# Two expert parts of 40 and 9 node tiles in place of 36, 12 and one tile computed densely

## The chip, the core and the metric

The kernel runs on one core of a Trainium2 chip. The metric is device time in microseconds (us), from launch to end, lower is better. The three timed runs shown took 4450.0 to 4450.73 us, their median is 4450.49 us.

## The reference

A stack of four layers works on 6250 nodes with 256 features and 106,250 edges, sorted by their target. Each layer reads a layer norm of `x` and adds its result to `x`: a graph convolution of the GIN kind, a slice attention, a GCN convolution, and a mixture of eight experts. The change touches the last one:

```
x_flat = x.reshape(-1, 256)
gate_logits = x_flat @ Wg + bg + bias                  # 6250 x 8
topk_vals, topk_idx = top_k(gate_logits, 2)
topk_w = softmax(topk_vals)
combine = (one_hot(topk_idx, 8) * topk_w[..., None]).sum(axis=1)
h = relu(einsum('td,edh->teh', x_flat, W1) + b1)       # W1: 8 x 256 x 512
y = einsum('teh,ehd->ted', h, W2) + b2                 # W2: 8 x 512 x 256
out = einsum('ted,te->td', y, combine)                 # two of eight experts count for each row
```

So for each row only two experts have a weight other than zero, and the kernel computes those two alone, except where the text below says otherwise.

## The kernel before

**Tiles.** Rows are taken in 49 tiles (NT) of 128 (P); the last one, tile 48, has 106 rows. An edge stage walks the tiles in order: GpSimd gathers 128 edge rows at a time (`msg`, L152; 831 gathers for each stage), VectorE builds 0/1 matrices (`hot`, L194), and TensorE sums the messages with three products each (`pa`, L173). The ring holds 10 gathered rows ahead. A tile's sum arrives in halves: each closes with row `s<-pa,ln` (L978) or L981.

**The third stage and its experts.** The GCN layer's sums and the experts share one loop (L1320 to L1342). While the sums of a tile run, seven slots (`between_products`, L1298) let other work in. A slot gives one step to the oldest *chain* (`choice`, L1004, one for two tiles) and half a block to the experts (`block_pieces`, L1280).

A chain makes the layer's output rows, normalizes them (`xn`), computes the gate logits (`pg`), picks two experts (L1042 to L1052), counts rows of each expert with two products (`pp`, L1075 and L1076), and so finds for every row two places in a table `XD` in DRAM (`place`). It takes seven steps. Then `send` (L1090) scatters the rows of `xn` to their places by indirect DMA from GpSimd, one for each tile and choice, and `advance` (L1118, some 28 small VectorE rows) works out which *blocks* of 128 rows of one expert are now full.

**Parts.** `XD` is divided into parts: part 0 has tiles 0 to 35, part 1 tiles 36 to 47. A part of T tiles has 2T + 7 blocks: 79 and 31. A block whose rows can't all be known before its part's last tile waits for it. So 18 blocks of each part become due only with its last `send`.

**A block.** `fetched` (L1170) loads on SP's queue the block's rows (`xd`) and its expert's weights (`weights_of`, L1159): W1 and W2 of 512 KB each, b1, and b2 as 128 KB. Up to four blocks are fetched ahead (AHEAD, L988), when a block ends or after a tile. `block_of` (L1206) transposes xd (`pt`, `xdT`), makes four column groups of the hidden layer (`ph`, L1195; `hT`, L1197) and the output (`py`, L1202; `yd`, L1203), and stores yd over the block's rows in `XD` (L1229).

**Combining.** Once all blocks of a part are stored, each of its tiles is combined: two indirect gathers (`g`, L1260) fetch its rows' two results, and two VectorE rows (L1265) add them to `xr` with their shares. The output store follows (`flush`, L1000). In the loop a tile is combined every eighth gather of msg (`beside`, L1270).

**The last tile.** Tile 48 belongs to no part. Its chain ends with its shares of all eight experts (`share`), and each expert is computed for the whole tile as one of eight *dense* blocks, without xd or a store; L1216 adds each to xr.

**The tail.** Behind the loop (L1343 on) what is left runs: the last `send`, the blocks still due, the dense blocks, with one step of the last chain and one tile's combining beside each half block; then what remains to be combined.

**Order.** SP, TensorE, ScalarE and VectorE run this stage in program order. GpSimd's indirect copies are kept in order by hand (`in_order`, L159). Thus a waiting instruction on SP holds back all loads and stores behind it, and one on GpSimd all gathers and scatters.

```
for upto, size in ((0.75, P), (1.0, P)):
    ts = [t for t in range(sum(map(len, parts)), NT - 1) if (t + 0.5) / (NT - 1) <= upto]
...
due.extend(fresh)
due.extend((None, e) for e in range(NE))
while due or ready or pending[0] is not None:
    next(last, None)
    next(block_pieces)
    if to_combine:
        combine(now[0] + 2)
    run_ends()
```

Of the kernel before, what the change touches and what calls it, by code (L numbers as in the profile page):

```python
# [9 lines left out]
F32 = mybir.dt.float32  # L10
# [3 lines left out]
OP = mybir.AluOpType  # L14
# [3 lines left out]
P = 128  # L18
# [3 lines left out]
def gin_transolver_gcn_moe(ctx: ExitStack, tc: tile.TileContext, a: dict, out: bass.AP):  # L22
# [13 lines left out]
    nc = tc.nc  # L36
    x, src, dst = a["x"], a["src"], a["dst"]
    N, D = x.shape
    E = src.shape[0]
    NT = -(-N // P)  # L40
# [17 lines left out]
    def rows_of(t):  # L58
        return min(P, N - t * P)
# [91 lines left out]
    def gather(msg, table, ix):  # L151
        return nc.gpsimd.indirect_dma_start(out=msg, out_offset=None, in_=table,  # L152
                                            in_offset=bass.IndirectOffsetOnAxis(ap=ix, axis=0))
# [217 lines left out]


    parts, Bs = [], []
    for upto, size in ((0.75, P), (1.0, P)):
        ts = [t for t in range(sum(map(len, parts)), NT - 1) if (t + 0.5) / (NT - 1) <= upto]
        if ts:
            parts.append(ts)
            Bs.append(size)
# [608 lines left out]

    TG, AHEAD = 2, 4  # L988
    outs = []
    share = keep.tile([P, NE], F32, name="share")  # L990
    s3s = {}

    def load_ahead(t):
# [10 lines left out]
    def choice(i, ts, sent_at):  # L1004
# [51 lines left out]
        def shares():  # L1056
            nc.scalar.activation(best[:, :J, 2], best[:, :J, 2], AF.Exp)
            nc.vector.tensor_scalar(best[:, :J, 3], best[:, :J, 2], 1.0, None, op0=OP.add)
            nc.vector.reciprocal(sh[:, :, 0], best[:, :J, 3])
            nc.vector.tensor_mul(sh[:, :, 1], best[:, :J, 2], sh[:, :, 0])  # L1060

        if i is None:
            shares()
            dense.append(xT)
            nc.vector.tensor_scalar(share, pick[0][:, 0, :], sh[:, 0, 0:1], None, op0=OP.mult)
            nc.vector.scalar_tensor_tensor(share, pick[1][:, 0, :], sh[:, 0, 1:2], share, op0=OP.mult, op1=OP.add)
            return


        both = w.tile([P, 4, NE], F32, name="both")  # L1070
        nc.vector.tensor_add(both[:, :J, :], pick[0][:, :J, :], pick[1][:, :J, :])
        yield
        yield
        pp = ps.tile([P, 2, 4, NE], F32, name="pp", tag="mm", bufs=3)
# [15 lines left out]
    def send(i, ts, xn):  # L1090

        for j, t in enumerate(ts):
            for c in range(2):
                ins = nc.gpsimd.indirect_dma_start(  # L1094
                    out=XD[i], out_offset=bass.IndirectOffsetOnAxis(ap=place[:, t, c:c + 1], axis=0),
                    in_=xn[:, j, :], in_offset=None)
                in_order(ins, False)
                for other in sent[i] + taken[i] + stored[i]:
                    tc.declare_no_dep(ins.ins, other, reason="no two rows go to one place")
                sent[i].append(ins.ins)  # L1100
        final = ts[-1] == parts[i][-1]
        which = advance(i, final)
        rows = 2 * P * (ts[-1] + 1 - parts[i][0])
        n = n_blocks[i] if final else max(0, -((NE * (Bs[i] - 1) - rows) // Bs[i]))
        fresh.extend((i, which, no, len(sent[i])) for no in range(n_due[i], n))
        n_due[i] = n
# [82 lines left out]
    def products(xdT, W1, W2, b1, b2):  # L1189

        hT = ew.tile([P, KH, P], F32, name="hT")
        for m in range(KH):
            p = ps.tile([P, 512], F32, name="ph", tag="mm", bufs=3)
            for k in range(KD):
                nc.tensor.matmul(p[:, :P], W1[:, k, m * P:(m + 1) * P], xdT[:, k, :P],  # L1195
                                 start=(k == 0), stop=(k == KD - 1))
            nc.scalar.activation(hT[:, m, :], p[:, :P], AF.Relu, bias=b1[:, m:m + 1])  # L1197
        yield
        yd = ew.tile([P, D], F32, name="yd")
        p = ps.tile([P, 512], F32, name="py", tag="mm", bufs=3)  # L1200
        for m in range(KH):
            nc.tensor.matmul(p[:, :D], hT[:, m, :], W2[:, m, :], start=(m == 0), stop=(m == KH - 1))  # L1202
        nc.vector.tensor_tensor(yd, p[:, :D], b2[:, 0, :], op=OP.add)  # L1203
        yield yd

    def block_of(i, got):  # L1206

        if i is None:
            e, got = got
            it = products(dense[0], *got)  # L1210
            next(it)
            yield
            yd = next(it)
            fetch_more()
            r, o = rows_of(NT - 1), xr[:, NT - 1, :]
            nc.vector.scalar_tensor_tensor(o[:r], yd[:r], share[:r, e:e + 1], o[:r], op0=OP.mult, op1=OP.add)  # L1216
            return
        fetch, r0, xd, *got = got
        pt = ps.tile([P, 512], F32, name="pt", tag="tr")
        for k in range(KD):  # L1220
            nc.tensor.transpose(pt[:, k * P:(k + 1) * P], xd[:, k * P:(k + 1) * P], ident)  # L1221
        xdT = ew.tile([P, KD, P], F32, name="xdT")
        nc.scalar.activation(xdT, pt[:, :D].rearrange("p (k n) -> p k n", k=KD), AF.Copy)
        yield
        it = products(xdT, *got)
        next(it)
        yield
        yd = next(it)
        ins = nc.sync.dma_start(XD[i][ds(r0, P), :], yd)  # L1229
        for other in taken[i]:  # L1230
            if other is not fetch:
                tc.declare_no_dep(ins.ins, other, reason="another block's rows")
        stored[i].append(ins.ins)
        fetch_more()
        left[i] -= 1
        if not left[i]:
            to_combine.extend((sums.n + CPT // 2, i, t) for t in parts[i])
# [2 lines left out]


    due, fresh, ready, left = [], [], [], {i: n for i, n in enumerate(n_blocks)}
    to_send, to_combine, dense, ends = [], [], [], []
    n_due = [0 for _ in parts]
    SLOTS = 7
    now = [0]
# [1 line left out]
    def fetch_more():  # L1248
        while len(ready) < AHEAD and due:
            b = due.pop(0)  # L1250
            ready.append((b[0], (b[1], weights_of(slice(b[1], b[1] + 1))) if b[0] is None else fetched(*b)))

    def combine(when):

        _, i, t = to_combine.pop(0)
        o = xr[:, t, :]
        gs = []
        for c in range(2):
            g = w.tile([P, D], F32, name="g", bufs=8)
            in_order(gather(g, XD[i], place[:, t, c:c + 1]))  # L1260
            gs.append(g)

        def end():
            for c in range(2):
                nc.vector.scalar_tensor_tensor(o, gs[c], share_of[:, t, c:c + 1], o, op0=OP.mult, op1=OP.add)  # L1265
            flush(4)
            outs.append((out[t * P:(t + 1) * P, :], o))
        ends.append((when, end))

    def beside(t):  # L1270
# [9 lines left out]
    def blocks():  # L1280

        while True:
            if pending[0] is not None:
                for _ in pending[0]:
                    pass
                pending[0] = None
            if ready:
                i, got = ready.pop(0)
                pending[0] = block_of(i, got)
                next(pending[0])  # L1290
                if i is not None:
                    yield
                    next(pending[0])
            yield

    block_pieces = blocks()
# [18 lines left out]
    def new_blocks():  # L1315
        due.extend(fresh)
        fresh.clear()
        fetch_more()

    sums.beside = beside  # L1320
    for i, ts_ in [*enumerate(parts), (None, [NT - 1])]:
        for q in range(0, len(ts_), TG):
            ts = ts_[q:q + TG]
            for t in ts:
                load_ahead(t)
                s = s3s[t]

                nc.vector.scalar_tensor_tensor(s, xr[:, t, :], ln3[:, 0, t:t + 1], s, op0=OP.mult, op1=OP.add)
                k = iter(range(SLOTS))

                def between():
                    n = next(k, None)
                    if n is not None:
                        between_products(t, n)

                now[0] = t * SLOTS
                sums(t, between, SLOTS)
                for n in k:
                    between_products(t, n)
                if t < NT - 1:  # L1340
                    new_blocks()
            chains.append(choice(i, ts, min(NCH, start(2 * ts[-1] + 2) + 3 * CPT // 2)))  # L1342
    last, = chains  # L1343
    for _, *rows in to_send:
        send(*rows)
    due.extend(fresh)
    due.extend((None, e) for e in range(NE))
    while due or ready or pending[0] is not None:
        next(last, None)
        next(block_pieces)  # L1350
        if to_combine:
            combine(now[0] + 2)
        run_ends()
    while to_combine or ends:
        if to_combine:
            combine(now[0] + 2)
        run_ends()
    outs.append((out[(NT - 1) * P:N, :], xr[:rows_of(NT - 1), NT - 1, :]))
    flush(0)
    late.close()  # L1360

# [22 lines left out]
```

## Time and profile before

| | us |
|---|---|
| median of the timed runs | 4450.49 |
| the profiled execution | 4515.05 |
| its span, first to last instruction | 4513.4 |
| GpSimd busy | 2578.6 (57%) |
| TensorE busy, matmul | 3133.2 (69%) |
| VectorE, ScalarE busy | 1532.2 (34%), 788.2 (17%) |
| msg gathers (L152), 2493 | 2359.7, 947 ns each |
| scatters XD<-xn (L1094), 96 | 94.7, 986 ns each |
| gathers g<-XD (L152), 96 | 93.8, 977 ns each |
| first row of stage 3's sums (L978) | 2800.6 |
| last msg gather starts | 4280.65 |

Times in the profile count from the first instruction. The profiled execution is longer than the timed runs, so shares and differences are read from it, not totals. Busy shares are means over stages with different limits; mean granted TensorE clock is 0.817 of full speed, mean DMA traffic 231 GB/s. A row is named by line, engine and operation, then output<-inputs by the program's names. In a bracket stands the idle time of the engine just before a row and what ended it.

### The profile page before, as it was taken

Reading aid. Unit: us, or ns where it says so; the run is one execution under the profiler, and the core shown is the slowest. Engines: PE = TensorE matmul, PEld = TensorE weight load, DVE = VectorE, ACT = ScalarE, POOL = GpSimd, SP = SyncE. Lnnn points to the kernel's source line nnn. Section 1 sums busy time; section 2 is a strip of 40 time slices with the busy share of each in tenths; the row PEclk is TensorE's granted clock in tenths of the full one; section 3 lists DMA queues with packets and bytes.
Section 4 is the critical chain, followed back from the end, with each engine's and each line's share of the span. In section 5 each row is a group of like instructions: output and inputs, shape, how many; then the busy total and the mean of one; then the engine's idle time right before and its main releaser. Section 6 shows DMA issues by size and latency. Waiting matters only on the chain. (4 is left out here: it accounts for less than half of the span.)

```text
span 4513.4 us, 45778 instructions
## 1 busy us (share of the span) xinstructions
PE 3133.2 (69%) x14516; PEld 2025.4 (45%) x14592; DVE 1532.2 (34%) x3891; ACT 788.2 (17%) x1496; POOL 2578.6 (57%) x2719
## 2 busy tenths in 40 slices
PE   2577777777874777878767876566666666677567
PEld 1233343433442444434434454345555555566456
DVE  6122222222231433433434454333333332333332
ACT  4011111111120111111111123011212221122122
POOL 3666666666646666666666502665665555555642
PEclk6688888888987898988989977677778777788779
DMA  6676666666668888888888755467766676687678
GB/s 210 190 227 215 215 197 206 210 214 208 195 210 289 296 295 301 304 293 289 297 289 292 248 165 178 136 189 220 225 206 207 216 222 215 215 263 219 194 239 257
DMA packets 497447, 1044.56 MB, mean 231 GB/s; under 512 B 79469, under 2 KB 294607, under 8 KB 497200
## 3 DMA queue, kind: packets, MB, share of 16 engines
q0 software_dynamic: 182064, 678.86, 47.8%
q1 hardware_dynamic: 308656, 353.08, 24.0%
q10 hardware_dynamic: 6480, 9.63, 0.6%
q8 instruction: 117, 1.92, 0.2%
q14 instruction: 130, 1.06, 0.1%
HBM read 878.42 MB, written 162.92 MB: 231 GB/s over the span
## 5 line engine op out<-in xcount | busy, mean ns | idle before, releaser
L152 POOL DMA_INDIRECT msg<-T,srcT x2493 | 2359.7, 947 | 1682.4 <-issue 763.0
L173 PE MATMUL pa<-msg,hot 128*128 128x256 bf16 (+2 forms) x7404 | 1492.0, 342 | 540.7 <-DMA msg<-T,srcT 395.1
L173 PEld LDWEIGHTS <-hot 128*128 128x128 bf16 x7479 | 804.8, 108 | 1142.0 <-issue 742.6
L1195 PE MATMUL ph<-xdT,W 128*128 128x128 f32 x1760 | 287.4, 315 | 197.6 <-ACT hT L1197 85.6
L194 DVE SCALAR_TENSOR_TENSOR hot<-dstT,node 128x1152 bf16<-128x1152 f32 (+2 forms) x297 | 373.1, 1258 | 23.8 <-PE pa L173 12.9
L1195 PEld LDWEIGHTS ph<-xdT,W 128*128 128x128 f32 x1760 | 252.8, 219 | 232.5 <-ACT hT L1197 97.5
L1202 PE MATMUL py<-W,hT 128*128 128x256 f32 x944 | 264.9, 425 | 25.4 <-issue 13.8
L622 DVE TENSOR_TENSOR dinv<-dinv,pa 128x1 f32<-128x1 f32 x145 | 22.3, 153 | 714.2 <-PE pa L173 460.8
L1197 ACT ACTIVATE hT<-ph,b1e 128x128 f32<-128x128 f32 x472 | 165.9, 367 | 449.7 <-remote 161.9
L835 PE MATMUL ptok<-xn,sw 128*128 128x257 f32 (+1 forms) x392 | 125.1, 458 | 157.1 <-DVE sw L827 63.7
L670 PE MATMUL p<-W2a,h2T 128*128 128x512 f32 x392 | 199.8, 651 | 33.9 <-issue 18.0
L1202 PEld LDWEIGHTS py<-W,hT 128*128 128x128 f32 x944 | 190.5, 215 | 64.8 <-issue 22.6
L663 PE MATMUL p<-h1T,W1b 128*128 128x512 f32 (+2 forms) x448 | 204.0, 599 | 19.5 <-ACT h1T L657 13.1
L835 PEld LDWEIGHTS ptok<-xn,sw 128*128 128x128 f32 (+1 forms) x392 | 84.8, 227 | 195.7 <-issue 74.7
L152 POOL DMA_INDIRECT g<-XD,place x96 | 93.8, 977 | 125.0 <-DMA XD<-yd 54.8
L1203 DVE TENSOR_TENSOR yd<-py,b2e 128x256 f32<-128x256 f32 x118 | 49.9, 423 | 306.6 <-PE py L1202 177.4
L1015 PE MATMUL pn<-Wg,sT 128*128 128x256 f32 x196 | 82.2, 592 | 83.6 <-issue 44.6
L655 PE MATMUL p<-h0T,W1a 128*128 128x512 f32 (+2 forms) x224 | 129.8, 711 | 7.3 <-issue 4.0
L663 PEld LDWEIGHTS p<-h1T,W1b 128*128 128x128 f32 x448 | 87.5, 212 | 103.8 <-issue 83.2
L670 PEld LDWEIGHTS p<-W2a,h2T 128*128 128x128 f32 x392 | 78.0, 211 | 121.6 <-issue 103.7
L1094 POOL DMA_INDIRECT XD<-xn,place x96 | 94.7, 986 | 62.5 <-issue 46.1
L235 DVE TENSOR_TENSOR s<-s,pa 128x512 f32<-128x512 f32 x49 | 33.6, 685 | 269.0 <-PE pa L173 146.7
(306 smaller groups left out, 3059.6 us busy)
## 6 DMA issues: line engine op xcount, KB each, us to landing
W<-in_L_ffn_W SPq DMA_DIRECT2D x236, 512.0 KB
XD<-zeros SPq DMA_DIRECT2D x100, 512.0 KB
msg<-T,srcT POOLq DMA_INDIRECT x2493
T<-tp SPq DMA_DIRECT2D x49, 384.0 KB
b2e<-in_L_ffn_b SPq DMA_DIRECT2D x118, 128.0 KB
xd<-XD SPq DMA_DIRECT2D x110, 128.0 KB
XD<-yd SPq DMA_DIRECT2D x110, 128.0 KB
S<-s SPq DMA_DIRECT2D x49, 256.0 KB
```

The source lines that it names most:

```text
L152: return nc.gpsimd.indirect_dma_start(out=msg, out_offset=None, in_=table, in_offset=bass.IndirectOffsetOnAxis(ap=ix, axis=0))
L173: nc.tensor.matmul(pa[:, :n], hot, msg[:, s * F:s * F + n], start=(start and s == 2), stop=(stop and s == 1))
L194: nc.vector.scalar_tensor_tensor(hot[:, :n, :], dstT[:, c0:c0 + n, None].to_broadcast([P, n, P]), float(k * HALF), node2[:, k % 2, None, : ...
L655: nc.tensor.matmul(p[:, :T], W1a[:, k, m * P:(m + 1) * P], h0T[:, k, :T], start=(k == 0), stop=(k == KD - 1))
L663: nc.tensor.matmul(p[:, :T], W1b[:, k, m * P:(m + 1) * P], h1T[:, k, :T], start=(k == 0), stop=(k == KH - 1))
L670: nc.tensor.matmul(p, h2T[:, k, j * P:(j + 1) * P], W2a[:, k, :], start=(k == 0), stop=(k == KH - 1))
L835: nc.tensor.matmul(p[:, :D + 1], sws[j][:r, m * P:(m + 1) * P], xn[:r, j, :], start=(j == 0), stop=(j == J - 1))
L1015: nc.tensor.matmul(p[:, :D], sT[:, k, j * P:(j + 1) * P], Wg3[:, k, :], start=(k == 0), stop=(k == KD - 1))
L1094: ins = nc.gpsimd.indirect_dma_start(out=XD[i], out_offset=bass.IndirectOffsetOnAxis(ap=place[:, t, c:c + 1], axis=0), in_=xn[:, j, :], in ...
L1195: nc.tensor.matmul(p[:, :P], W1[:, k, m * P:(m + 1) * P], xdT[:, k, :P], start=(k == 0), stop=(k == KD - 1))
L1197: nc.scalar.activation(hT[:, m, :], p[:, :P], AF.Relu, bias=b1[:, m:m + 1])
L1202: nc.tensor.matmul(p[:, :D], hT[:, m, :], W2[:, m, :], start=(m == 0), stop=(m == KH - 1))
```

## The change

Parts are formed over all 49 tiles, with a limit of 0.81: part 0 has tiles 0 to 39, part 1 tiles 40 to 48. The numbers of blocks become 87 and 25, the dense blocks are gone. The last tile's chain is a chain like all others; rows past the 106 count as zero in `both`, and its scatters, gathers, sums and output store have 106 rows. In the tail, all chains that are left take one step in each round, and one waiting `send` is made in a round, after which its blocks are fetched at once.

```diff
-    for upto, size in ((0.75, P), (1.0, P)):
-        ts = [t for t in range(sum(map(len, parts)), NT - 1) if (t + 0.5) / (NT - 1) <= upto]
+    for upto, size in ((0.81, P), (1.0, P)):
+        ts = [t for t in range(sum(map(len, parts)), NT) if (t + 0.5) / NT <= upto]
...
-        if i is None:
-            shares()
-            dense.append(xT)
-            nc.vector.tensor_scalar(share, pick[0][:, 0, :], sh[:, 0, 0:1], None, op0=OP.mult)
-            nc.vector.scalar_tensor_tensor(share, pick[1][:, 0, :], sh[:, 0, 1:2], share, op0=OP.mult, op1=OP.add)
-            return
...
-        nc.vector.tensor_add(both[:, :J, :], pick[0][:, :J, :], pick[1][:, :J, :])
+        r = rows_of(ts[-1])
+        if r < P:
+            nc.vector.memset(both[:, :J, :], 0.0)
+            if J > 1:
+                nc.vector.tensor_add(both[:, :J - 1, :], pick[0][:, :J - 1, :], pick[1][:, :J - 1, :])
+            nc.vector.tensor_add(both[:r, J - 1, :], pick[0][:r, J - 1, :], pick[1][:r, J - 1, :])
+        else:
+            nc.vector.tensor_add(both[:, :J, :], pick[0][:, :J, :], pick[1][:, :J, :])
...
+            r = rows_of(t)
             for c in range(2):
                 ins = nc.gpsimd.indirect_dma_start(
-                    out=XD[i], out_offset=bass.IndirectOffsetOnAxis(ap=place[:, t, c:c + 1], axis=0),
-                    in_=xn[:, j, :], in_offset=None)
+                    out=XD[i], out_offset=bass.IndirectOffsetOnAxis(ap=place[:r, t, c:c + 1], axis=0),
+                    in_=xn[:r, j, :], in_offset=None)
...
-        if i is None:
-            e, got = got
-            it = products(dense[0], *got)
...
-            nc.vector.scalar_tensor_tensor(o[:r], yd[:r], share[:r, e:e + 1], o[:r], op0=OP.mult, op1=OP.add)
-            return
...
-            in_order(gather(g, XD[i], place[:, t, c:c + 1]))
-            gs.append(g)
+            in_order(gather(g[:r], XD[i], place[:r, t, c:c + 1]))
+            gs.append(g[:r])
...
-    for i, ts_ in [*enumerate(parts), (None, [NT - 1])]:
+    for i, ts_ in enumerate(parts):
...
-                if t < NT - 1:
-                    new_blocks()
+                new_blocks()
...
-    last, = chains
-    for _, *rows in to_send:
-        send(*rows)
-    due.extend(fresh)
-    due.extend((None, e) for e in range(NE))
-    while due or ready or pending[0] is not None:
-        next(last, None)
+    while chains or to_send or due or ready or pending[0] is not None:
+        for it in list(chains):
+            if next(it, chains) is chains:
+                chains.remove(it)
+        if to_send:
+            send(*to_send.pop(0)[1:])
+            new_blocks()
         next(block_pieces)
         if to_combine:
             combine(now[0] + 2)
...
-    outs.append((out[(NT - 1) * P:N, :], xr[:rows_of(NT - 1), NT - 1, :]))
```

More of the change, by code (lines that the diff above doesn't have):

```diff
@@ L989, in gin_transolver_gcn_moe @@
     outs = []
-    share = keep.tile([P, NE], F32, name="share")
     s3s = {}
@@ L1206, in block_of @@
     def block_of(i, got):
-        if i is None:
-            e, got = got
-            it = products(dense[0], *got)
[L1211 to L1215, printed above, removed]
-            nc.vector.scalar_tensor_tensor(o[:r], yd[:r], share[:r, e:e + 1], o[:r], op0=OP.mult, op1=OP.add)
-            return
         fetch, r0, xd, *got = got
@@ L1242, in gin_transolver_gcn_moe @@
     due, fresh, ready, left = [], [], [], {i: n for i, n in enumerate(n_blocks)}
-    to_send, to_combine, dense, ends = [], [], [], []
+    to_send, to_combine, ends = [], [], []
     n_due = [0 for _ in parts]
@@ L1250, in fetch_more @@
             b = due.pop(0)
-            ready.append((b[0], (b[1], weights_of(slice(b[1], b[1] + 1))) if b[0] is None else fetched(*b)))
+            ready.append((b[0], fetched(*b)))
     def combine(when):
         _, i, t = to_combine.pop(0)
-        o = xr[:, t, :]
+        r = rows_of(t)
+        o = xr[:r, t, :]
         gs = []
@@ L1259, in combine @@
             g = w.tile([P, D], F32, name="g", bufs=8)
-            in_order(gather(g, XD[i], place[:, t, c:c + 1]))
-            gs.append(g)
+            in_order(gather(g[:r], XD[i], place[:r, t, c:c + 1]))
+            gs.append(g[:r])
         def end():
             for c in range(2):
-                nc.vector.scalar_tensor_tensor(o, gs[c], share_of[:, t, c:c + 1], o, op0=OP.mult, op1=OP.add)
+                nc.vector.scalar_tensor_tensor(o, gs[c], share_of[:r, t, c:c + 1], o, op0=OP.mult, op1=OP.add)
             flush(4)
-            outs.append((out[t * P:(t + 1) * P, :], o))
+            outs.append((out[t * P:t * P + r, :], o))
         ends.append((when, end))
@@ L1290, in blocks @@
                 next(pending[0])
-                if i is not None:
-                    yield
-                    next(pending[0])
+                yield
+                next(pending[0])
             yield
```

## The prediction

> **What bounds the kernel now.** I read three views of the last sixth of the run: the start of row s<-pa,ln (L978, one per node tile), stage windows, and the timelines of SP and POOL. From tile 8 on, the third aggregation runs with three expert blocks beside one tile and one beside the next; from 3019.5 to 3951.8 us thirty such tiles take 932.3 us, 31.08 each. The program order of TensorE and the starts of yd<-py (L1203) give the blocks between them: 89 before the last product of row pa at 4300 us, 29 behind it.
>
> ```profile
> 4117.14 0.48 DVE L978 SCALAR_TENSOR_TENSOR s<-pa,ln,s 128x256 f32<-128x256 f32 x1 [1.71 <-PE pa L173]
> 4263.13 0.47 DVE L978 SCALAR_TENSOR_TENSOR s<-pa,ln,s 128x256 f32<-128x256 f32 x1
> 4303.07 0.48 DVE L978 SCALAR_TENSOR_TENSOR s<-pa,ln,s 128x256 f32<-128x256 f32 x1
> ```
>
> These are tiles 43, 47 and 48 (columns: start, length). Tiles 43 to 46 take 146.0 us, 36.5 each, with nine blocks only; tiles 38 to 42, with seventeen, took 165.3, 33.1 each. The four are those beside which the g gathers of part 0 run (nine tiles' pairs up to tile 47).
>
> The stage windows of the last 561.6 us (columns: stretch, length, busy us of PE, PEld, DVE, ACT and POOL, then granted clock, DMA share and GB/s):
>
> ```profile
> 3951.80:4117.10 165.30, 127.65 (x782) 108.64 (x780) 58.22 (x222) 43.04 (x105) 90.59 (x96) 0.87 0.81 252
> 4117.10:4263.10 146.00, 91.16 (x520) 74.16 (x520) 48.72 (x169) 25.95 (x60) 86.85 (x93) 0.76 0.64 195
> 4263.10:4303.10 40.00, 22.45 (x102) 17.30 (x99) 13.16 (x52) 7.47 (x14) 14.22 (x15) 0.63 0.71 219
> 4303.10:4345.30 42.20, 26.10 (x118) 22.32 (x118) 15.83 (x66) 10.79 (x26) 23.29 (x24) 0.70 0.62 193
> 4345.30:4406.10 60.80, 43.46 (x208) 35.53 (x208) 17.46 (x41) 14.59 (x40) 29.77 (x31) 0.80 0.89 276
> 4406.10:4460.60 54.50, 47.50 (x270) 38.92 (x269) 8.63 (x20) 18.71 (x51) 3.40 (x4) 0.97 0.92 281
> 4460.60:4513.40 52.80, 28.34 (x159) 24.96 (x157) 17.84 (x40) 9.36 (x26) 24.27 (x24) 0.83 0.74 235
> ```
>
> See that the tail from 4303.1 us has no gathers of msg, yet takes 210.3 us: it is the blocks that were left. Once it runs (rows five and six) DMA is 0.89 to 0.92 busy, so transfers set its pace. SP and POOL show its two edges:
>
> ```profile
> 4295.78 0.51 SPq L1002 DMA_DIRECT2D out<-xr  x1
> 4311.35 0.34 SPq L1229 DMA_DIRECT2D XD<-yd  x1
> 4317.74 0.72 SPq L1177 DMA_DIRECT2D xd<-XD  x1
> 4322.01 0.69 SPq L1161 DMA_DIRECT2D W<-in_L_ffn_W  x1
> ```
> ```profile
> 4409.47 0.95 POOL L152 DMA_INDIRECT g<-XD,place  x1 [0.30 <-issue]
> 4465.18 0.94 POOL L152 DMA_INDIRECT g<-XD,place  x1 [54.76 <-DMA XD<-yd]
> ```
>
> Between 4294.8 and 4322.0 us no weight is asked for: SP first waits for a block's yd, then xd waits for the last scatters (POOL, the last of them at 4307.38). And part 1's combining starts at 4465.18 us, 4.6 us behind the last store of yd (4460.59); the eight dense blocks run beside its 24 gathers.
>
> **The change, part by part.** *In the loop.* Blocks before the last pa stay 89, but part 0 ends at tile 40, so its backlog (17 blocks in five tiles) moves from tiles 38 to 42 to tiles 42 to 46, its last blocks are done at the loop's end, and no g gather is left in the loop. Tiles 38 to 41: 4 x 31.08 = 124.3; tiles 42 to 46: 165.3 as measured for the same blocks; tile 47 kept at 40.0 (it has two blocks for one, but loses a combined tile). Sum for tiles 38 to 46: 289.6 against 311.3, **21.7 us less**. I take all the excess of tiles 43 to 46 as the combining's; what else it could be is the second rival. Bounds: 5 and 32 less (32 if tile 47 too falls to 33).
>
> *Tail, start.* Block 92 (the fourth of the tail) has its yd at 4345.32, 42.2 us in. The fetch of 92 now stands ahead of the store of 89 on SP, so it waits for the scatters alone: a gain of 0 to 8. But tile 48 is scattered too: the fetch of block 96 waits on SP for its two scatters, and behind it stand all later weights, stores and outputs, hence every later block. Its chain ended at 4335.6 us before; the prefix product, place and POOL's two scatters come one block later, some 4348, landed some 10 us on (4307.38 to 4317.74 at the first such wait). Four blocks are in hand, and 23.3 us pass from W's issue to yd (4322.01 to 4345.32): cost 0 to 8. The two are set against each other: 0.
>
> *Tail, middle.* All 40 tiles of part 0 are now combined here, one per half block, so 20 blocks have gathers beside them. Such a block took (4406.09 - 4345.32) / 8 = 7.6 us; one without (yd 4418.76 to 4445.49, five blocks) 5.3. Blocks 93 to 107: 15 x 7.6 = 114.0. The last four have no weights left to load: 4 x 5.3 = 21.2. The last yd is at 42.2 + 114.0 + 21.2 = 177.4, its store 0.4 later.
>
> *Tail, end.* Nothing runs beside part 1's combining: 4.6 for the store to land, 17 gathers at 1.25 (0.95 and 0.30 issue), and from the last gather's start to the end 9.7 as now (4503.66 to 4513.4): 35.6. A gather's buffer is awaited only eight on (bufs 8), 10 us, so the gathers don't wait for DVE.
>
> *106 rows.* The rule that speaks against the change: the Trainium skill, "DMA: Bandwidth & Descriptors", section "Why a DMA increments its semaphore by 16 and not by 1", lets a copy use the largest number of engines up to 16 that divides the rows; for 106 that is 2. The trace agrees for the store of the last tile's output:
>
> ```profile
> 4508.90:4511.70 2.80, 0.00 (x0) 0.00 (x0) 0.00 (x0) 0.00 (x0) 0.00 (x0) 0.50 0.13 37
> ```
>
> 0.13 of 16 engines at 37 GB/s, where 128-row rows had 276. That store is last in both kernels. But the scatters and gathers of tile 48 are new copies of 106 rows. By the g row of 128 they cost nothing extra; by the rule each last gather takes some 2.5 us longer (108.5 KB at 37 GB/s is 2.9). No 106-row indirect copy is in the trace (the page names an exception for some copies from POOL); by shape the store is nearest: **+2**, ends 0 and 5.
>
> So the tail is 177.8 + 35.6 + 2 = 215.4 against 210.3: **5.1 us more**. That six blocks fewer (118 to 112; each 1.18 MB of weights and b2e, 4.3 us at 276 GB/s) don't shorten it: 24 of the g gathers and outputs of loop tiles move in, the dense blocks' cheap pace (eight in 40 us) goes, and the end has no cover.
>
> *Costed at nothing:* one more advance on DVE (4303.47 to 4307.59, 4.1 us) and the memset and add into both, DVE being busy 29% in the tail; without that cover, 5. Removed: ten small DVE rows of the dense part, ACT's 24 hT rows, hidden as well. Fills of XD grow from 100 to 102, each 0.5 MB, in the first stage beside gathers: 0, at most 5 if its DMA (0.66 busy) were the limit.
>
> Sum: -21.7 + 5.1 = -16.6 on the profiled 4515.05 us (span 4513.4). The runs' median, 4450.49, is 1.4% shorter than the profiled execution; scaled, -16.4: **4434.1**.
>
> **Rivals.**
> - *More gain:* tile 47 falls to 33 (-7), and the tail's middle runs at 6.4 as blocks 92 to 96 (6.7) and 99 to 102 (5.9) did on average (15 x 1.2 = 18 less): 41 less, 4410. Against it: 276 GB/s in the middle window.
> - *No loop gain:* tiles 44, 46 and 47 are long for late weights (TensorE idled 12.9 us before ph in tile 44) and low clock (0.76, 0.63), not for combining. Then tiles 42 to 46 take 36.5 each, 182.5 + 124.3 = 306.8, 4.5 less; with the tail's +5.1: 4451, no change. For it: a g pair is 2.5 us of POOL, POOL was 0.59 busy there. Against: these are the only long tiles.
> - *Slower, the second gate:* SP's hold for tile 48's scatters isn't covered but repeats the first one in full, 27.2 us from weight to weight (4294.8 to 4322.0), in a tail that DMA paces. -16.6 + 27.2 = +10.6: 4461. It takes back all gain from 16.6, and decides for slower from 25.5. For it: yd's gap of 19.6 us at the first gate (blocks 89 to 90). Against: then 22 us passed with the fetch queue not filled, now four blocks are fetched first.
> - *Not what it says:* excluded; the two programs' order on TensorE shows 118 blocks to 112 and 29 to 23 behind the last pa.
>
> **Numbers.** 0.2% (8.9 us) is about what a measurement of this kernel can tell from no change. Forecast 0.58 (0.52 faster, 0.05 same, 0.01 slower); more gain 0.14, all faster; no loop gain 0.15 (0.10 same, 0.05 slower, if a gate comes on top); second gate 0.13 (0.03 same, 0.10 slower). So faster 0.66, same 0.18, slower 0.16. Forecast's own range 4420 to 4448; to hold the rivals but for their outer halves, 4412 to 4462.
>
> **What would show it.** Right: no g row before the last msg gather; tiles 38 to 41 at 31 and 42 to 46 at 33 us; last pa 20 us earlier; the last store of yd 178 us behind tile 48's L978; the end 36 us behind that store. Wrong: tiles 42 to 46 at 36 or more; a gap of weights on SP over 15 us a second time; gathers g waiting at the end; blocks beside combining at over 8 us.

## The result, and the profile after

The changed kernel takes 4438.17 us (median of 20 runs, 4412.16 to 4473.14) beside 4456.67 us for the kernel before (20 runs, 4444.54 to 4475.54). The medians differ by 18.5 us. The comparison's own ratio is 0.9956, 95% interval [0.9937, 0.9974]: 19.6 us less, between 11.6 and 28. The forecast was 16.4 us less.

The profiled execution of the changed kernel took 4425.39 us (span 4423.7, mean clock 0.831). It can't be set against the 4515.05 us of before as a whole: 32 of the 89.7 us between the two spans lie ahead of stage 3, where only two fills of `XD` were added (2800.6 us to its first sum before, 2768.6 now). Another 30 lie in tiles 8 to 37, whose work is the same (31.08 us a tile before, 30.07 now). So the stages are compared, and even they are read from an execution that ran 3% faster where nothing was changed.

Starts of L978 in the changed kernel, tiles 43, 47 and 48 (columns: start, length):

```profile
4052.11 0.48 DVE L978 SCALAR_TENSOR_TENSOR s<-pa,ln,s 128x256 f32<-128x256 f32 x1 [0.78 <-PE pa L173]
4177.72 0.48 DVE L978 SCALAR_TENSOR_TENSOR s<-pa,ln,s 128x256 f32<-128x256 f32 x1 [2.54 <-remote]
4214.24 0.48 DVE L978 SCALAR_TENSOR_TENSOR s<-pa,ln,s 128x256 f32<-128x256 f32 x1
```

Tiles 43 to 46 now take 125.6 us for 146.0, and tile 47 36.5 for 40.0. The stage windows of the changed kernel (stretch, length, busy us of PE, PEld, DVE, ACT and POOL, granted clock, DMA share, GB/s): tiles 38 to 41, tiles 42 to 46, tile 47, the tail to yd of block 92, to block 107, to the last store, the end, and the last output's transfer alone:

```profile
3899.10:4018.80 119.70, 79.71 (x476) 65.61 (x476) 43.09 (x157) 24.60 (x56) 72.63 (x76) 0.81 0.70 218
4018.80:4177.70 158.90, 122.33 (x776) 106.06 (x776) 58.65 (x222) 43.47 (x105) 89.69 (x94) 0.88 0.83 256
...
4177.70:4214.20 36.50, 25.48 (x141) 20.88 (x140) 10.82 (x45) 8.83 (x18) 12.28 (x13) 0.73 0.73 222
4214.20:4253.50 39.30, 26.38 (x133) 23.21 (x134) 19.60 (x98) 12.02 (x29) 18.90 (x19) 0.79 0.56 170
4253.50:4364.60 111.10, 76.64 (x397) 63.06 (x395) 32.73 (x77) 26.89 (x76) 65.66 (x68) 0.88 0.93 296
4364.60:4387.60 23.00, 16.81 (x86) 13.70 (x86) 5.62 (x13) 5.86 (x17) 0.00 (x0) 0.93 0.78 245
4387.60:4423.70 36.10, 0.00 (x0) 0.00 (x0) 8.72 (x18) 0.00 (x0) 18.26 (x18) 0.54 0.41 119
4418.20:4422.50 4.30, 0.00 (x0) 0.00 (x0) 0.45 (x1) 0.00 (x0) 0.00 (x0) 0.50 0.09 25
```

See that the backlog of part 0 (second row) runs at 31.8 us a tile with TensorE the busiest, that the tail's middle (fifth row) stands at 0.93 of DMA and 296 GB/s, and that of the compute engines only GpSimd and VectorE work in the last 36 us.

SP's queue at the two gates, the waits for scatters:

```profile
4204.77 0.38 SPq L1163 DMA_DIRECT2D W<-in_L_ffn_W  x1
...
4207.23 0.36 SPq L1219 DMA_DIRECT2D XD<-yd  x1
4222.38 0.71 SPq L1177 DMA_DIRECT2D xd<-XD  x1
4224.52 0.00 SPq L1161 DMA_DIRECT2D W<-in_L_ffn_W  x1
...
4252.85 0.34 SPq L1165 DMA_DIRECT2D b1e<-B  x1
4253.40 0.59 SPq L1167 DMA_DIRECT2D b2e<-in_L_ffn_b  x1
4260.82 0.70 SPq L1177 DMA_DIRECT2D xd<-XD  x1
4261.63 0.38 SPq L1161 DMA_DIRECT2D W<-in_L_ffn_W  x1
4263.68 0.71 SPq L1163 DMA_DIRECT2D W<-in_L_ffn_W  x1
4267.25 0.69 SPq L1165 DMA_DIRECT2D b1e<-B  x1
4271.44 0.00 SPq L1167 DMA_DIRECT2D b2e<-in_L_ffn_b  x1
4272.14 0.70 SPq L1001 DMA_DIRECT2D out<-xr  x1
4274.24 0.69 SPq L1219 DMA_DIRECT2D XD<-yd  x1
...
4278.77 0.00 SPq L1161 DMA_DIRECT2D W<-in_L_ffn_W  x1
```

The fetch of block 92 stands ahead of stores and leaves at 4222.38; no weights were asked for in 19.7 us (4204.77 to 4224.52). The second gate is there too: the fetch of block 96 leaves at 4260.82, and the store of block 92's yd, ready at 4253.9, leaves only at 4274.24. What that costs is seen at VectorE's row of block 94:

```profile
4275.69 0.42 DVE L1203 TENSOR_TENSOR yd<-py,b2e 128x256 f32<-128x256 f32 x1 [6.56 <-remote]
```

It waits for two things. The tile yd has two buffers, so block 94 needs the one that block 92's store reads. And TensorE's py of this block, which by the profile's model ends at 4268.55, updates its semaphore only at 4275.67. Both engines are slow in this stretch; the last section returns to it.

GpSimd's two scatters of tile 48, and its last gathers:

```profile
4249.32 1.57 POOL L1094 DMA_INDIRECT XD<-xn,place  x1 [14.76 <-ACT hT L1197]
4251.20 1.57 POOL L1094 DMA_INDIRECT XD<-xn,place  x1 [0.31 <-issue]
...
4390.31 0.95 POOL L152 DMA_INDIRECT g<-XD,place  x1 [26.73 <-DMA XD<-yd]
...
4410.31 1.57 POOL L152 DMA_INDIRECT g<-XD,place  x1 [0.30 <-issue]
4412.19 1.56 POOL L152 DMA_INDIRECT g<-XD,place  x1 [0.30 <-issue]
```

The second gate's rows were sent at 4251.20. Part 1's combining starts 2.7 us behind the last store (4387.6), and goes, with never more than the usual 0.30 us between gathers, to the two gathers of 106 rows, which keep GpSimd for 1.57 us each in place of 0.95.

### The profile page after: what moved, and what is told of

It reads as the page before. It is cut to its first block, busy times and chain, and to the rows that moved or that the text cites. A ratio compares the mean times of both kernels' runs of the same rounds, so it can differ in the third digit from the quotient of the medians.

```text
span 4423.7 us, 45587 instructions
## 1 busy us (share of the span) xinstructions
PE 3063.0 (69%) x14455; PEld 1970.8 (45%) x14456; DVE 1531.8 (35%) x3910; ACT 780.1 (18%) x1474; POOL 2587.1 (58%) x2723
## 5 line engine op out<-in xcount | busy, mean ns | idle before, releaser
L173 PE MATMUL pa<-msg,hot 128*128 128x257 bf16 (+2 forms) x7479 | 1494.5, 340 | 567.9 <-DMA msg<-T,srcT 473.0
L1202 PE MATMUL py<-W,hT 128*128 128x256 f32 x896 | 238.5, 411 | 14.4 <-ACT hT L1197 7.9
L1202 PEld LDWEIGHTS py<-W,hT 128*128 128x128 f32 x896 | 174.9, 207 | 44.5 <-ACT hT L1197 11.3
L815 PE MATMUL pl<-Weff,xnT 128*128 128x512 f32 x196 | 112.9, 664 | 24.8 <-issue 13.9
L236 DVE TENSOR_TENSOR s<-s,pa 64x512 f32<-64x512 f32 x48 | 33.2, 692 | 249.1 <-PE pa L173 114.2
```

The source lines that it names most:

```text
L173: nc.tensor.matmul(pa[:, :n], hot, msg[:, s * F:s * F + n], start=(start and s == 2), stop=(stop and s == 1))
L815: nc.tensor.matmul(p, xnT[:, k, j * P:(j + 1) * P], Weff[:, k, :], start=(k == 0), stop=(k == KD - 1))
```

## The experiments

Twelve experiments ran, in three groups, each timed beside the kernel before: its median is 4532.69 us (59 runs) in the first group, 3991.35 (43 runs) in the second, 4524.52 (52 runs) in the third. The record doesn't tell which chip a group ran on. Ratios are to before in the same group. The stages below come from one profile each; groups one and three are close in pace and stand together, with the two first profiles. "Sum" is from tile 38 to the end, and "end" from the last store of yd (with dense blocks, that end also holds them).

| kernel | tiles 38-46 | tile 47 | tail | of it end | sum |
|---|---|---|---|---|---|
| before (first profile) | 311.3 | 40.0 | 210.3 | 52.8 | 561.6 |
| b_copy (before) | 307.8 | 40.6 | 210.8 | 52.2 | 559.2 |
| after (first profile) | 278.6 | 36.5 | 209.5 | 36.1 | 524.6 |
| a_again (after) | 296.7 | 38.3 | 225.5 | 36.0 | 560.5 |
| a_third (after) | 291.4 | 39.7 | 217.8 | 36.2 | 548.9 |
| b_tail_combine | 290.3 | 38.7 | 222.3 | 56.2 | 551.3 |
| b_tail_combine_wf | 279.3 | 37.2 | 220.3 | 55.0 | 536.8 |
| b_40_8_dense | 288.9 | 41.2 | 218.9 | 49.7 | 549.0 |
| a_36_13 | 305.4 | 39.9 | 217.0 | 46.0 | 562.3 |
| a_wf_g128 | 293.7 | 38.2 | 222.9 | 32.4 | 554.8 |

Read the three rows of the changed kernel first: their sums differ by 36 us, more than the change brings. One profile shows where a stage's time goes, not whether the kernel is faster; for that the timed ratios stand. Means agree with them (before 560.4, after 544.7, 15.7 us less), but this is weak support: with such a spread the mean of three sums is known to some 10 us (an estimate from the three), so that the agreement is in part luck.

**a_again and a_third: the changed kernel once more.** No edit.

> The changed kernel once more, as a yardstick beside the next three. Theory (combining moved out of the loop): about 0.9956 of before; tiles 42 to 46 near 1.06 of the ordinary tiles, tail some 210 us, 36 us of it after the last store. Any rival expects the same total.

> The changed kernel unchanged, beside the three others on their chip, as their base. Expected from its two earlier comparisons (0.9956 and 0.9972): ratio to before 0.995 to 0.998. If what the change does depends on the chip, it falls outside.

Measured: 4521.75 us, ratio 0.9972 [0.9952, 0.9991], and 4509.27 us, 0.9966 [0.9948, 0.9983]. With 0.9956 that is three comparisons, each faster, by 12.7 to 19.6 us. Each is known to some 9 us either way, and so are the other ratios of groups one and three.

**b_tail_combine: the kernel before, but no tile is combined in the loop.**

```diff
-        if n % (CPT // 2) == 0 and to_combine and to_combine[0][0] <= n:
-            combine(t * SLOTS + (n - start(2 * t)) * SLOTS // CPT + 2)
```

> The kernel before, but no tile is combined in the loop: all 36 of part 0 wait for the tail, nothing else changes. Theory (combining beside the sums made tiles 43 to 46 long): these four fall from 36.5 to 31 or 32 us each, 20 us less; nine more tiles combined beside tail blocks cost 9 x 1.15 = 10 us; total 10 us less, 0.998 of before. Rival (late weights and a low clock made them long): they stay at 36, total 10 us more, 1.002. Rival (fewer blocks are the whole gain): no faster than before, 1.000 to 1.002.

Measured: 4523.66 us, ratio 0.9958 [0.9938, 0.9979] (the two plain medians give 0.9980, which lies outside the comparison's interval; for the changed kernel beside it they give 0.9976, and the comparison 0.9972). The size is thus uncertain between 9 and 19 us. By either reading two lines taken away, with the old parts and the dense last tile, do as well as the whole change, within what these runs can tell.

**b_copy: the kernel before, for its stages.** No edit.

> The kernel before, unchanged: one profile on the chip of the three others, so that the tiles beside which the second results are gathered can be set against an ordinary tile of the same execution. Theory A (GpSimd's queue, 18 gathers of 1.25 us): tiles 43 to 46 are 20 to 27 us longer than four times the mean of tiles 8 to 37, whatever the chip's pace. Theory B (late weights and low clock): the excess follows the chip, and is under 12 us on a chip where the core runs at 3990 us.

Stage windows of b_copy (as above), tiles 38 to 42 and 43 to 46:

```profile
3969.00:4134.40 165.40, 125.97 (x780) 107.64 (x777) 58.49 (x222) 42.97 (x105) 89.56 (x94) 0.87 0.79 249
4134.40:4276.80 142.40, 91.63 (x518) 75.73 (x519) 48.56 (x170) 26.10 (x61) 87.52 (x93) 0.77 0.65 201
```

The same windows of b_tail_combine:

```profile
3988.20:4156.70 168.50, 126.40 (x780) 107.53 (x778) 58.60 (x223) 43.35 (x106) 90.50 (x96) 0.87 0.77 242
4156.70:4278.50 121.80, 87.44 (x502) 71.58 (x503) 43.65 (x158) 25.73 (x61) 72.63 (x77) 0.80 0.70 216
```

Both have the same blocks beside the same tiles. See POOL's column: 93 indirect copies against 77, 16 gathers of g less, and 20.6 us less for the four tiles. By the queue's pace, 0.95 us and 0.30 to the next, 16 gathers are 20.0. Over two profiles each it is 144.2 (146.0, 142.4) against 121.45 (121.8, and 121.0 in b_tail_combine_wf). b_copy's own test was set between the tiles and an ordinary tile (31.29 in that execution): 142.4 less four of these is 17.2 us, between the two theories' numbers, and in a group of the slower pace; so it doesn't tell whether the excess follows the chip. The ordinary tile was a poor base, since without gathers the four run below it (30.4 each).

What GpSimd waited for in these windows, in b_copy and in b_tail_combine (columns: us, times, longest):

```profile
POOL msg L152 <- PE pa L173: 15.7, 13, 4.2
...
POOL msg L152 <- PE pa L173: 17.1, 14, 4.3
```

So GpSimd waits for TensorE to free a buffer of the ring about as long with the gathers as without them, and is idle for 54.9 of 142.4 us in b_copy. A queue with that much idle time need not have charged the gathers' whole time. That it did is measured; how, these profiles don't show.

**b_sp_loads: combining stays in the loop, but SP loads as many bytes in place of its 18 gathers.** The rows loaded are not those that are meant, so those nine tiles' outputs are not the reference's.

```diff
-            in_order(gather(g, XD[i], place[:, t, c:c + 1]))
+            if plain:
+                nc.sync.dma_start(g, XD[i][c * P:(c + 1) * P, :])
+            else:
+                in_order(gather(g, XD[i], place[:, t, c:c + 1]))
```

> The kernel before, but in the loop a tile's two results are loaded by SP from fixed rows of XD in place of two gathers by GpSimd; these nine tiles' output is not the reference's. The bytes, the sums on VectorE and the output stores stay. Theory A (18 gathers at 1.25 us of GpSimd's queue, 22.5 us, stand in the way of msg gathers): tiles 43 to 46 fall to 31 or 32 us each, as without combining in the loop. Theory B (the traffic, VectorE's rows or SP's stores lengthen them): they stay at 36.

Measured: 3977.41 us, ratio 0.9969 [0.996, 0.9978]. Stage window of b_sp_loads, tiles 43 to 46:

```profile
3642.20:3745.90 103.70, 79.04 (x498) 64.60 (x499) 47.84 (x170) 25.38 (x58) 69.69 (x73) 0.84 0.86 274
```

103.7 us, four ordinary tiles of this execution (25.98 each) being 103.9. In the two profiles of before the same tiles were 1.17 and 1.14 times four ordinary ones (31.08 and 31.29). The bytes, VectorE's additions and the outputs are all still there (POOL's count alone is lower), so it isn't the traffic or VectorE's rows that lengthen the tiles but the gathers as GpSimd's copies. Two things stay open. SP loads rows that lie together, so the gathers' turn in the queue and their scattered rows are not told apart. And in this group, of which there is no profile of before, the timed gain is 12.4 us (8.8 to 16.0), less than the 22.8 above: either the gathers cost less at this pace, or SP's loads cost something.

**b_40_8_dense: the kernel before with parts of 40 and 8, the last tile still dense.**

```diff
-    for upto, size in ((0.75, P), (1.0, P)):
+    for upto, size in ((0.83, P), (1.0, P)):
```

> The kernel before with parts of 40 and 8 tiles, the last tile still computed densely by eight blocks: only the division is changed. Theory: the loop gains its 21 us, the tail has 13 more tiles to combine beside blocks (15 us more) and four fewer at the end (5 us less): 10 to 12 us less in all, 0.9975 of before, so that scattering the last tile adds the rest. Rival (six blocks fewer are the whole gain): 1.000 or more. Rival (the division is all): 0.9956.

Measured: 4525.21 us, ratio 0.998 [0.9961, 0.9998]. No gather of g is left in its loop either (the first at 4296.1 us), and its tiles 38 to 46 are as short as the changed kernel's. Its interval overlaps that of the changed kernel beside it; whether the dense last tile costs anything is not told apart.

**a_36_13: the changed kernel with parts of 36 and 13, so that combining is in the loop again.**

```diff
-    for upto, size in ((0.81, P), (1.0, P)):
+    for upto, size in ((0.74, P), (1.0, P)):
```

> The changed kernel with parts of 36 and 13 tiles: the last tile is scattered, 112 blocks, 23 of them in the tail, but nine tiles of part 0 are combined in the loop again. Theory: the loop is 20 us longer than in the changed kernel, the tail the same within 5 us (9 tiles less beside blocks, 4 more at the end): 1.000 of before, within 0.002. Rival (fewer blocks are the whole gain): 0.9956 as the changed kernel.

Measured: 4532.78 us, ratio 0.9993 [0.9969, 1.0018]. With the gathers back in the loop (the first at 4149.2 us), nothing is left of the gain, though the last tile is scattered, six blocks are saved and all chains advance together. Tiles 43 to 46 take 143.6 us in its profile.

**a_42_7: the changed kernel with the limit 0.85, parts of 42 and 7.**

```diff
-    for upto, size in ((0.81, P), (1.0, P)):
+    for upto, size in ((0.85, P), (1.0, P)):
```

> The changed kernel with parts of 42 and 7 tiles: 112 blocks, 24 of them in the tail, still no combining in the loop, 14 gathers at the end for 18. Theory: one more block in the tail costs 7 us, two tiles more beside blocks 2, two fewer at the end save 5, catching up two tiles later saves 4 in the loop: the same as the changed kernel within 5 us. Rival (the end without cover is the price of the tail): 5 us less or more. Rival (blocks in the tail are the price): 8 us more.

Measured: 3978.23 us, ratio 0.9969 [0.9959, 0.9978], in the second group; end 31.4 us with 14 gathers in place of 18, 24 blocks in the tail. A division further on has about the ratio that the changed kernel has in the other groups (0.9956 to 0.9972). This fits the view that what counts is on which side of the loop's end the combining falls, but the changed kernel wasn't timed in this group.

**a_gather128: the last tile's gathers take all 128 rows.**

```diff
-            in_order(gather(g[:r], XD[i], place[:r, t, c:c + 1]))
+            in_order(gather(g, XD[i], place[:, t, c:c + 1]))
```

> The changed kernel, but the last tile is fetched for combining with gathers of 128 rows, of which the last 22 are not used. Theory (a 106-row indirect copy runs on two DMA engines): the two last gathers take 0.95 instead of 1.57 us on GpSimd, the last of them lands some 2.5 to 3 us sooner after its start (5.7 us before), and the end behind the last store is 33 us instead of 36. Rival (only the number of rows differs): 36 us as before.

One execution, 3970.81 us. Its last two gathers on GpSimd:

```profile
3959.27 0.95 POOL L152 DMA_INDIRECT g<-XD,place  x1 [0.30 <-issue]
3960.52 0.95 POOL L152 DMA_INDIRECT g<-XD,place  x1 [0.30 <-DVE xr L1256]
```

VectorE's last row in a_gather128:

```profile
3963.59 0.48 DVE L1256 SCALAR_TENSOR_TENSOR xr<-g,share_of,xr 106x256 f32<-106x256 f32 x1 [0.91 <-DMA g<-XD,place]
```

And the last row in the changed kernel:

```profile
4418.16 0.48 DVE L1256 SCALAR_TENSOR_TENSOR xr<-g,share_of,xr 106x256 f32<-106x256 f32 x1 [1.02 <-DMA g<-XD,place]
```

From the last gather's start to VectorE it is 3.07 us with 128 rows (3960.52 to 3963.59) and 5.97 with 106 (4412.19 to 4418.16); in the third group alone 3.09 (a_wf_g128) and 5.97 (a_third). The end is 32.4 us, also in a_wf_g128 of the third group, against 36.0 to 36.2 in four profiles with 106 rows, one of them of this group: 3.7 us. In the changed kernel only GpSimd's queue has packets in this stretch, those of the last gather (columns as in the stage windows):

```profile
4416.50:4417.40 0.90, 0.00 (x0) 0.00 (x0) 0.48 (x1) 0.00 (x0) 0.00 (x0) 0.50 0.12 50
```

0.12 of 16 engines is two.

**a_weights_first: a block's W1 and W2 are asked for ahead of its rows.**

```diff
+        W = weights_of(ds(e, 1))
         xd = ew.tile([P, D], F32, name="xd", bufs=AHEAD)
...
-        return (ins.ins, r0, xd) + weights_of(ds(e, 1))
+        return (ins.ins, r0, xd) + W + biases_of(ds(e, 1))
```

> The changed kernel, but each fetch asks for W1 and W2 ahead of the block's rows xd, so that SP waits for a part's scatters only behind 1 MB of weights. Theory (SP's wait for scatters delays weights: 19.7 and 15.1 us without a weight at the two gates of the tail, and TensorE idles 5 to 10 us before ph in every second tile of the loop): the gaps between weights at the gates fall under 12 us, the tail is 8 to 15 us shorter, an ordinary tile 0.5 to 1 us shorter, the total 20 to 40 us less than the changed kernel. Rival (the transfers themselves set the pace, or xd now comes late behind its own weights): same as the changed kernel or up to 15 us slower.

Measured: 3963.95 us (6 runs), ratio 0.9932 [0.9911, 0.9952]. It looked faster than all others, from few runs and without the changed kernel beside it. So it ran once more with the gathers of 128 rows, beside the changed kernel:

> The changed kernel with both of the small edits tried alone before: each block's weights are asked for ahead of its rows, and the last tile's gathers take 128 rows. Theory A (weights first lets the weights pass the two waits of the last scatters; gathers of 128 rows land from 16 engines, not 2): 0.4% less than the changed kernel beside it, ratio to before 0.992 to 0.9935; end behind the last store of yd 32 to 33 us for 36. Theory B (what weights first gained was the scatter of one comparison of few runs): ratio within 0.001 of the changed kernel's but for the 3.6 us of the end (0.0009), so 0.995 to 0.9965.

Measured: 4507.34 us, ratio 0.9962 [0.9945, 0.9979]; the changed kernel beside it 0.9966. That is theory B: the end is 3.8 us shorter, and no more is seen. It does little for the second gate: block 96's weights are asked for ahead of the wait, but block 97's stand behind it and leave 62.7 us into the tail, against 64.5 to 66.6 in the three profiles of the changed kernel. Whether it gains at the second group's pace is open; the changed kernel wasn't timed there.

**b_tail_combine_wf: the kernel before, no combining in the loop, and weights first.**

> The kernel before (parts of 36 and 12, dense last tile) with only two edits: no tile is combined in the loop, and each block's weights are asked for ahead of its rows. Theory A (nearly all of the change's gain is the gathers that leave the loop; parts of 40 and 9 and the scattered last tile bring nothing of their own): as fast as the changed kernel with both small edits, within 0.002, ratio to before 0.992 to 0.996. Theory B (the division matters: six blocks fewer, 7 MB of weights less in a tail that transfers pace): slower than it by over 0.003, ratio 0.996 to 0.998.

Measured: 4503.02 us, ratio 0.9958 [0.9939, 0.9977], 0.0004 from a_wf_g128. Theory A: with the gathers out of the loop, the old parts and the dense last tile are as fast, within the intervals. No version timed beside the changed kernel beats it by more than these.

## Why the prediction was right

**Loop: right, also in its reason.** -21.7 us were forecast for tiles 38 to 46 and none for tile 47. The means of the profiles are 309.6 before and 288.9 after, -20.7, and tile 47 fell from 40.3 to 38.2. The step rested on taking all the excess of tiles 43 to 46 as the combining's. With the combining alone taken away they lose 22.8 us; with SP carrying it, in the second group, they are ordinary tiles. The rival of late weights and low clock falls with that: the granted clock of these tiles was still 0.80 without the gathers (0.77 in b_copy), not the 0.87 of the stretch before, and the excess was gone all the same. What spoke for the step's smaller bound, that POOL is only 0.6 busy there, was no guide: the gathers cost at least their own 1.25 us each. Why the idle time took in none of it stays open.

**Tail, start and second gate: the two did not cancel.** The gain at the first gate and the cost of the second were set against each other at 0. The gain came: weights were missing for 19.7 to 23.5 us (28.9 and 31.8 in the two profiles of before, from 4293.07 and not from 4294.8, where b2 was asked for), and yd of block 92 stood at 39.3, 40.8 and 41.1 us for 42.2. The second gate took back more. Yd of block 94 came 12.6, 14.5 and 14.6 us behind the one before, 5.0 to 7.0 more than the 7.6 forecast for a block. As the prediction had it, the four blocks in hand covered the wait itself: behind it TensorE waits for no weights. What cost the time is a slow stretch of SP and TensorE, which the prediction didn't know of. In a_gather128, whose order is the same and which has no such stretch, block 94 came only 7.0 us behind. The rival of the gate in full, 27.2 us, falls.

**Tail, middle: right but for that block.** 7.6 us a block were forecast; 7.41, 8.51 and 7.84 were measured, mean 7.9, so 4.8 us over 15 blocks. Without block 94 the mean is 7.5. Two signs that were named for a wrong forecast did show at the edge: a second gap of weights of 15.1 us in the first profile (4263.68 to 4278.77; 14.6 in the others), and over 8 us a block in a_again. The last four blocks took 21.5, 20.5 and 21.5 (21.2 forecast). The rival with 6.4 a block falls.

**Tail, end: right, from errors that offset each other.** 35.6 and 2 were forecast, 36.1 measured. The first gather came 2.7 us behind the last store, not 4.6, and from the last gather to the end 8.6 us pass with 128 rows, not 9.7. The 106 rows cost 3.7 us, not 2: the slower landing was foreseen from the store of the last output (0.13 of 16 engines at 37 GB/s while its packets ran) and from the rule in the Trainium skill, "DMA: Bandwidth & Descriptors", section "Why a DMA increments its semaphore by 16 and not by 1", by which 106 rows go to two engines. The runs agree for GpSimd's indirect copies too: two engines are at work, and it is 2.9 us longer to the sum (5.97 against 3.07), where some 2.5 were worked out. But 0.6 us of it, and of the gather before, is time on GpSimd, which was not foreseen. Ends of 0 and 5 held it.

**The sum.** Loop with tile 47 -22.8 and tail +7.0 (210.6 to 217.6 in the means) make -15.8; forecast -16.6. That it comes so close is in part luck, given the spread of the profiles and errors of 1 to 5 us in the tail that offset each other. That six blocks less and the end of the dense blocks would not pay by themselves held too: a_36_13 has both and is no faster than before.

## What to carry to other kernels

Copies slipped into an in-order queue that feeds a loop can cost their whole time, even where its busy share is 0.6: here 16 gathers cost some 23 us in four tiles of the loop, and all 18 cost some 11 us in the tail, so they belong behind the loop. When a change does several things, take out the one mechanism that carries the sum and run it alone: two deleted lines did as well as the whole change, within some 9 us. Don't judge a change of 0.4% by one profile: three of the same kernel differed by 36 us over their last eighth.

## What was not expected of the hardware

- Indirect copies of 106 rows hold GpSimd for 1.57 us, gathers and scatters alike, where gathers of 128 rows take 0.95 and scatters 0.97 to 1.00.
- SP issues slowly behind the second gate: from the fetch of block 96 to the store of yd, seven issues took 13.4 us (4260.82 to 4274.24), with 2 to 4 us between most of them, where b1 and b2 follow each other by 0.55 us just ahead (4252.85 to 4253.40). More of the second gate is this than the wait itself (7.4 us, 4253.40 to 4260.82). In this stretch even SP's register moves take 0.70 us, where their median is 0.03, and TensorE's semaphores come late.
- Such stretches are no matter of the gate. In the ten profiles of the slower pace (the first two, groups one and three) they come about every second tile of stage 3, and 61 to 73 of SP's 660 to 672 moves there take 0.6 to 0.8 us. In the four profiles of the second group none does. They don't make the excess of tiles 43 to 46: by this count those have 7 and 4 slow moves with the gathers, and 6 and 6 without. Their cause stays open.
- The groups differ far more than the two kernels: 3991 us in the second, 4525 and 4533 in the others and 4457 in the first comparison, all for the kernel before. Gathers of msg take 946 to 949 ns in all, but an ordinary tile takes 26.0 to 26.2 us in the second group, without the slow stretches, and 30.1 to 31.5 in the other profiles, with them. Mean DMA traffic is 261 to 263 GB/s there and 229 to 235 in the others, the granted clock 0.85 to 0.86 against 0.82 to 0.83. Whether this is another chip or another state of one is not on record.
